# Cross-attention, 32 batches: in each window of the main loop the query products come first and third and the output products second and fourth, their two PSUM banks change places, and one query copy moves into the first softmax exponentials

## The chip, the cores and the metric

The kernel runs on one core of a Trainium2 chip. The metric is device time in microseconds (us) of one execution. The kernel before takes 1692.46 us, the median of three runs (1692.12 to 1692.76).

The core has a matrix engine (PE; its weight loads are listed apart as PEld), a vector engine (DVE), an activation engine (ACT), a general engine (POOL) and a queue that issues DMAs (SP). Each works through its own instructions in the order in which they stand. They wait for one another by semaphores.

## The reference: what is computed

```python
q = _heads(hidden_states @ to_q_w)
h_txt = _sdpa(q, _heads(ehs_txt @ to_k_w), _heads(ehs_txt @ to_v_w))
...
out = out @ to_out_w + to_out_b
out = (out + residual) / RESCALE
```

`x` is 32 batches of 512 rows by 640 columns, the context 32 batches of 77 rows by 1024. The attention has 20 heads of width 32. The context has only 77 rows, so the three further attentions of the source get empty slices and nothing of them is left: one attention, its output product, bias and residual are what must be computed. All is float32.

## The kernel before

**Pieces.** The 640 columns are cut into five pieces of 128 (four heads each). One *slot* is one piece of one batch, so there are N = 160 slots; slot n belongs to batch n // 5. A large product is made of 15 matmuls of 128x512: five pieces k of the inner dimension, and for each k three products of high and low parts (both operands are split into a rounded high part and the rest, the low part). The order is the same for every k: high·high, then weight high by **data low**, then weight low by data high (`PAIRS`). Counted from 0, matmul 3k+1 is the first to need the low part of piece k of the data.

**Stages.** A first part (about 320 us) makes keys and values of all batches and works off slots 0 to 7. The main loop, `window(n)`, then takes two slots at a time, n = 8, 10, ... 158: 76 windows. The position w = n % 10 says which batch work a window does beside its own, since two batches are ten slots.

**A window.** On PE stand, in this order:
- `values(n-4)` into bank `po` and `values(n-3)` into bank `pq` (L553): probabilities times values.
- `scores_of_two(n)` (L454): 64 small matmuls into the four `sc` banks and two `pa` banks.
- four large products of 15 matmuls: `group(early)` (L602, output product of slot n-8 into `po`), `queries(n+2)` (L437, into `pq`), `group(later)` (L602, into `po`), `queries(n+3)` (L437, into `pq`).

ACT casts the high parts of the two value results (`high_a`, L567), makes 32 exponentials with their sums (`exps`, L515), and copies the query product of slot n+2 to `qt` (`copy_q`, L449). DVE makes low parts (`low_a`, L572), row maxima (L508), the transposes of an output product (`turn`, L612), the reciprocal of the sums (L525), the transpose of the probabilities (`transpose_p`, L534) and the query copy of slot n+3 (L449). POOL multiplies the probabilities by the reciprocals (`normalize`, L527), adds output products to the residual (`add`, L616, after `turn`), adds the bias (`bias_of`, L587) and makes the low parts of x (`split_x`, L259, whose high part ACT casts in L258). SP issues `move_p` (L543) and the loads and stores.

**Batch work by position.** `split_x` makes the query operand `xt` of a batch, five pieces c = 0 to 4, at three places:
- w = 6: pieces 0 and 1 of batch b+2, late in the window.
- w = 8: pieces 2 to 4 of batch b+2, at the window's start. The first query product that reads them is `queries(n+2)` of this same window, since n+2 is the first slot of that batch.
- w = 2: pieces 0 and 1 of batch b+1 ahead of the exponentials, pieces 2 to 4 behind `normalize(n)`. The first query product that reads them is `queries(n+3)` of this same window.

`bias_of` runs in windows with w = 0, 4, 6 and 8. No scheduler moves anything: the order of each engine is the order in which the code calls the helpers.

Of the kernel before, what the change touches and what calls it, by code (L numbers as in the profile page):

```python
# [37 lines left out]
def kernel(  # L38
# [25 lines left out]
    nc = tc.nc  # L64
# [4 lines left out]
    NC_ = C // P  # L69
# [3 lines left out]
    N = B * NC_  # L73
# [176 lines left out]
    def split_x(b, c, high=nc.scalar.copy, low=nc.gpsimd):  # L250

        if b == 1 and c > 1:
            xt = xpool[1].tile([P, 2, S], FPR, tag="xu", name="xu", bufs=3)
        else:
            xt = xpool[0].tile([P, 2, S], FPR, tag="xt", name="xt", bufs=7)
        src = xss[b].rearrange("p (a t) u -> p t a u", t=NQ)[:, :, :, c * Q : (c + 1) * Q]
        parts = [xt[:, i, :].rearrange("p (t a j) -> p t a j", t=NQ, j=Q) for i in range(2)]
        high(parts[0], src)  # L258
        low.tensor_tensor(parts[1], src, parts[0].bitcast(F32), ALU.subtract)  # L259
        xts[b, c] = xt  # L260
# [26 lines left out]
    early = kvt.tile([P, P], F32, name="early", bufs=1)  # L287
# [144 lines left out]
    def queries(n, tag="pq"):  # L432
        b, j = divmod(n, NC_)
        pqs[n] = bank(tag)
        for k in range(NC_):
            for m, (a, c) in enumerate(PAIRS):
                nc.tensor.matmul(  # L437
                    pqs[n],
                    wq_s[:, k, a, j * P : (j + 1) * P],
                    xts[b, k][:, c, :],  # L440
                    start=(k == 0 and m == 0),
                    stop=(k == NC_ - 1 and m == 2),
                )
# [4 lines left out]
    def copy_q(n, copy=nc.scalar.copy):  # L448
        copy(qt_of(n), pqs.pop(n))  # L449
# [73 lines left out]
    def normalize(n):  # L523
        rs = main.tile([P, NQ * HPC], F32, tag="rs", name="rs", bufs=2)
        nc.vector.reciprocal(rs, sms.pop(n))  # L525
        pf = pnb[n % 2][:, :, :NKEY]
        nc.gpsimd.tensor_tensor(  # L527
            pf, pf, rs.unsqueeze(2).to_broadcast([P, NQ * HPC, NKEY]), ALU.mult
        )
# [18 lines left out]
    def values(n, tag="pa"):  # L548
        b, j = divmod(n, NC_)
        raw, vb = raws.pop(n), vbs[b % 2][:, j]  # L550
        pas[n] = bank(tag)
        for i in range(HPC):
            nc.tensor.matmul(  # L553
                pas[n][i * HD : (i + 1) * HD, :].rearrange("p (a q) -> p a q", q=P),
                vb[:, i, :],
                raw[:, :, i, :],
                start=True,
                stop=True,
                tile_position=(0, i * HD),
            )  # L560
# [35 lines left out]
    def group(b, c, ks, tag="po"):  # L596

        for k in ks:
            if k == 0:
                pos[b, c] = bank(tag)  # L600
            for m, (a, d) in enumerate(PAIRS):
                nc.tensor.matmul(  # L602
                    pos[b, c],
                    wos[0][:, k, a, c * P : (c + 1) * P],
                    ats[b * NC_ + k][:, d, :],
                    start=(k == 0 and m == 0),
                    stop=(k == NC_ - 1 and m == 2),
                )

    def turn(b, c):  # L610
        ots[b, c] = late[0].tile([P, S], F32, tag="ot", name="ot", bufs=2)
        nc.vector.transpose(ots[b, c], pos.pop((b, c)))  # L612

    def add(b, c):
        part = ys[b][:, :, c * Q : (c + 1) * Q]
        nc.gpsimd.tensor_tensor(  # L616
            part, part, ots.pop((b, c)).rearrange("p (a i) -> p a i", i=Q), ALU.add
        )
# [39 lines left out]
    def take(m, tag="pa"):  # L658
        values(m, tag)
        high_a(m)  # L660
        low_a(m)
# [65 lines left out]
    def window(n):  # L727

        w, b = n % 10, n // 10 * 2
        ahead = n + 2 < N  # L730
        taken = (n - 4, n - 3)
        early, later = (divmod(n - FIRST + i, NC_) for i in range(2))
        for m in taken:
            values(m, "pq" if m == n - 3 else "po")
        for m in taken:
            high_a(m)
        normalize(n - 1)
        for m in taken[:-1]:
            low_a(m)
        views, shared = scores_of_two(n)  # L740
        low_a(n - 3)
        for i in range(3):
            maxima_of(views[i], i)
        transpose_p(n - 1)
        maxima_of(views[3], 3)
        move_p(n - 2)
        if w == 8 and b:
            store_y(b - 1, range(4))
        if w == 8 and b + 2 < B:
            for c in range(2, NC_):  # L750
                split_x(b + 2, c)
        if w == 2:
            for c in range(2):
                split_x(b + 1, c)
        for i in range(HPC):
            exps(n, i)
        group(*early, range(NC_))
        turn(*early)
        for i in (1, 3):
            maxima_of(shared[i], i, 6)  # L760
        add(*early)
        move_p(n - 1)
        if w == 0:
            load_values(b)
            load_keys(b + 1)
            load_y(b - 1, range(4))
        if w == 2 and b > 1:
            store_y(b - 2, range(4))
        if w == 4:
            load_values(b + 1)  # L770
            if b + 2 < B:
                load_x(b + 2)
        if w == 6:
            if b + 2 < B:
                load_keys(b + 2)
            load_y(b, range(4))
        if w == 8 and b + 3 < B:
            load_x(b + 3)
        if ahead:
            queries(n + 2)  # L780
        normalize(n)
        if n == N - 10:
            nc.gpsimd.dma_start(biases[0], bo.unsqueeze(0).to_broadcast([P, C]))
        if w in BIAS and b >= BIAS[w][0]:
            for i in BIAS[w][1]:
                bias_of(b - BIAS[w][0], i)
        for i in (0, 2):
            exps(n + 1, i, range(2, NQ))
        if ahead:
            copy_q(n + 2)  # L790
        if w == 2:
            for c in range(2, NC_):
                split_x(b + 1, c)
        if w in (0, 6) and b + w // 6 + 1 < B:
            for i in range(NQ):
                transpose_x(b + w // 6 + 1, i)
        transpose_p(n)
        for i in (1, 3):
            exps(n + 1, i, range(2, NQ))
        for i in (1, 3, 0, 2):  # L800
            if i == 0 and w == 6 and b + 2 < B:
                for c in range(2):
                    split_x(b + 2, c)
            if i == 0 and not ahead:
                closing(n)
            exps(n + 1, i, range(2))
        if ahead:
            group(*later, range(NC_))
            turn(*later)
            add(*later)  # L810
            queries(n + 3)
            copy_q(n + 3, nc.vector.tensor_copy)

    def closing(n):

        last = B - 1
        for t in range(NQ):
            load_residual(t)
        for c, tag in ((1, "pq"), (2, "po")):
            group(last - 1, c, range(NC_), tag)  # L820
            turn(last - 1, c)
            add(last - 1, c)
        values(n - 2, "pq")
        high_a(n - 2)

    def end():


        last = B - 1
        low_a(N - 4)  # L830
        move_p(N - 2)
        normalize(N - 1)
        take(N - 3, "po")
        for c, tag in ((3, "pq"), (4, "po")):
            bias_of(last - 1, c - 2)
            group(last - 1, c, range(NC_), tag)
            turn(last - 1, c)
            if c == 3:
                transpose_p(N - 1)
                move_p(N - 1)  # L840
            add(last - 1, c)
        bias_of(last - 1, 3)
        store_y(last - 1, range(4))
        for t in range(NQ):
            add_bias(t)

        def begin(i, ks=range(4)):
            t, h = divmod(i, 2)
            if 0 in ks:
                pos[t, h] = bank(("sc", "sc", "sc", "sc", "pq", "po", "pa", "pa")[i])  # L850
            for k in ks:
                project(t, h, k)

        def close(t):
            for h in range(2):
                project(t, h, 4)
                finish(t, h)

        for i in range(4):
            begin(i, range(3))  # L860
        for m in (N - 2, N - 1):
            take(m)
        for i in (4, 5):
            begin(i, range(3))
        for i in range(6):
            begin(i, (3,))
        close(0)
        close(1)
        begin(6)
        close(2)  # L870
        begin(7)
        close(3)
# [68 lines left out]
```

## Time and profile before

| | |
|---|---|
| median of three runs | 1692.46 us |
| the profiled execution | 1692.86 us |
| its span (first to last instruction) | 1690.8 us |
| PE busy (matmuls) | 1683.6 us, 12460 matmuls |
| ACT busy | 1075.9 us |
| DVE busy | 1010.5 us |
| POOL busy | 990.1 us |
| one window at position w = 8 (n = 88), start to start | 17.63 us |

The profile is of one execution. A timeline row gives the start, the time until the last instruction of the row ends, the engine, the line, the operation, what is written and read, and how many instructions the row joins; in brackets stands the idle time of the engine ahead of it and what ended that. Two neighbouring instructions of one engine overlap a little, so the distance of two starts says better than the length how long an engine is taken. PE's busy time counts modelled ends and hides short waits; there too the distance of starts is read.

### The profile page before, as it was taken

The numbers are of one execution on the slowest core, as the hardware profiler recorded it, in microseconds if no ns is written. First come the engines' busy times: TensorE is split into PE (matmuls) and PEld (weight loads), VectorE is DVE, ScalarE is ACT, GpSimd is POOL, SyncE is SP. The second block draws the span as 40 slices with busy tenths as digits, with TensorE's granted clock in tenths as the row PEclk, the third lists the DMA queues.
The fourth block names the chain that finished last, engine by engine and source line by source line (L and its number), as shares of the span: only waits on it lengthen the run. The fifth ranks groups of instructions, "written<-read, shape, count | busy, mean of one in ns | idle before, by whom it ended". The sixth has DMA issues, their size and how long they took to land.

```text
span 1690.8 us, 36827 instructions
## 1 busy us (share of the span) xinstructions
PE 1683.6 (100%) x12460; PEld 1303.9 (77%) x12460; DVE 1010.5 (60%) x1635; ACT 1075.9 (64%) x5622; POOL 990.1 (59%) x663
## 2 busy tenths in 40 slices
PE   9999999999999999999999999999999999999999
PEld 7888898777777777777777777777777777777777
DVE  4341235766676666766666657576666766667653
ACT  3231125867677676776767767677676776767762
POOL 1000026667667666667575766767667676766755
PEclk9999999999999999999999999999999999999999
DMA  9847558678889787879797988888979788888956
GB/s 182 159 94 189 121 103 229 150 173 188 190 187 204 172 204 175 202 181 212 166 211 166 211 181 195 185 194 186 203 173 204 173 202 190 188 192 183 210 136 187
DMA packets 363852, 306.51 MB, mean 181 GB/s; under 512 B 88784, under 2 KB 292112, under 8 KB 363664
## 3 DMA queue, kind: packets, MB, share of 16 engines
q1 hardware_dynamic: 360864, 296.61, 78.4%
q0 software_dynamic: 2704, 7.38, 1.4%
q8 instruction: 99, 1.62, 0.4%
q14 instruction: 89, 0.73, 0.1%
q10 hardware_dynamic: 96, 0.16, 0.0%
HBM read 120.36 MB, written 57.88 MB: 105 GB/s over the span
## 4 chain that ended last, share of the span: by engine, by line
PE 97%; DMA 1%; ACT 0%; DVE 0%; SPq 0%; issue 0%; POOL 0%; DVEq 0%; ACTq 0%
PE pq L437 32%; PE po L602 31%; PE pv L182 7%; PE pk L182 7%; PE sc L454 6%; PE po L553 4%; PE pq L553 4%; PE pa L454 3%; DMA wraw<-in_L_xattn_to_k_w_dram 1%; PE sc L634 1%; PE pa L553 0%; ACT pn L515 0%; DMA cs<-in_ctx_dram 0%; PE pa L634 0%; PE pq L602 0%; SPq L99 0%
## 5 line engine op out<-in xcount | busy, mean ns | idle before, releaser
L515 ACT ACTIVATE pn<-sc,nm 128x77 f32<-128x77 f32 x1928 | 597.3, 367 | 131.4 <-DVE nm L508 102.8
L437 PE MATMUL pq<-xt,wq_s 128*128 128x512 f32 x2349 | 559.0, 390 | 0.0
L602 PE MATMUL po<-at,wo_s 128*128 128x512 f32 x2295 | 554.6, 393 | 0.0
L437 PEld LDWEIGHTS pq<-xt,wq_s 128*128 128x128 f32 x2349 | 440.6, 188 | 91.4
L602 PEld LDWEIGHTS po<-at,wo_s 128*128 128x128 f32 x2295 | 425.1, 188 | 90.8
L515 ACT ACTIVATION_READ_ACCUMULATOR pn<-sc,nm 128x1 f32 x1928 | 477.3, 249 | 0.0
L527 POOL TENSOR_TENSOR pn<-pn,rs 128x1232 f32<-128x1232 f32 x160 | 363.6, 2273 | 125.3 <-DVE rs L525 121.8
L616 POOL TENSOR_TENSOR xs<-xs,ot 128x512 f32<-128x512 f32 x155 | 199.8, 1289 | 322.1 <-DVE ot L612 314.4
L534 DVE STREAM_TRANSPOSE z<-pn 128x1536 f32<-128x1536 f32 x160 | 282.3, 1765 | 113.7 <-POOL pn L527 92.2
L259 POOL TENSOR_TENSOR xt<-xs,xt 128x512 fp32r<-128x512 f32 x157 | 198.5, 1293 | 35.8 <-ACT xt L258 35.8
L515 ACT ACTIVATE pn<-pa,nm 128x77 f32<-128x77 f32 x620 | 200.5, 382 | 0.0
L587 POOL TENSOR_TENSOR xs<-xs,bias_y 128x640 f32<-128x640 f32 x124 | 192.4, 1574 | 0.2
L567 ACT CAST at<-po 128x512 fp32r<-128x512 f32 x77 | 45.1, 585 | 230.1 <-PE po L553 230.1
L508 DVE TENSOR_REDUCE nm<-sc 128x6 f32<-128x462 f32 x304 | 177.1, 624 | 15.2 <-PE pa L454 15.2
L449 DVE COPY qt<-pq 128x512 f32<-128x512 f32 x83 | 57.4, 691 | 210.1 <-PE pq L437 210.1
L454 PE MATMUL sc<-kb,qt 32*128 32x77 f32 x3856 | 161.9, 273 | 0.0
L515 ACT ACTIVATION_READ_ACCUMULATOR pn<-pa,nm 128x1 f32 x620 | 161.0, 263 | 0.0
L454 PEld LDWEIGHTS sc<-kb,qt 32*128 32x128 f32 x3856 | 149.4, 187 | 4.2 <-issue 2.2
L182 PE MATMUL pk<-ct,wk_s 128*128 128x512 f32 (+1 forms) x600 | 134.0, 382 | 0.7 <-ACT wk_s L89 0.5
L182 PE MATMUL pv<-ct,wv_s 128*128 128x512 f32 (+1 forms) x600 | 134.2, 382 | 0.0
L454 PEld LDWEIGHTS pa<-kb,qt 32*128 32x128 f32 x1240 | 83.9, 186 | 63.7 <-ACT at L567 63.7
L182 PEld LDWEIGHTS pk<-ct,wk_s 128*128 128x128 f32 x600 | 112.1, 188 | 20.9 <-ACT wk_s L89 1.2
(81 smaller groups left out, 1339.7 us busy)
## 6 DMA issues: line engine op xcount, KB each, us to landing
raw<-z SPq DMA_DIRECT2D x640, 192.0 KB, 3.4
xs<-in_x_dram SPq DMA_DIRECT2D x256, 320.0 KB, 6.3
out_dram<-xs SPq DMA_DIRECT2D x127, 320.0 KB, 4.8
vb<-v_dram SPq DMA_DIRECT2D x32, 240.0 KB, 4.4
kb<-k_dram SPq DMA_DIRECT2D x32, 192.5 KB, 4.6
cs<-in_ctx_dram SPq DMA_DIRECT2D x12, 512.0 KB, 9.0
k_dram<-ks POOLq DMA_DIRECT2D x20, 256.0 KB, 2.5
v_dram<-vs SPq DMA_DIRECT2D x80, 64.0 KB, 2.4
```

Of the source, the lines that this page charges most:

```text
L182: nc.tensor.matmul(held[j][:, :gn], w[:, k, a, :], cts[g, k][:, c, :gn], start=(k == 0 and n == 0), stop=(k == NK - 1 and n == 2),)
L259: low.tensor_tensor(parts[1], src, parts[0].bitcast(F32), ALU.subtract)
L437: nc.tensor.matmul(pqs[n], wq_s[:, k, a, j * P : (j + 1) * P], xts[b, k][:, c, :], start=(k == 0 and m == 0), stop=(k == NC_ - 1 and m == 2),)
L454: nc.tensor.matmul(out, qt_of(n)[r, t * P : (t + 1) * P], kbs[b % 2][r, j, :], start=True, stop=True, tile_position=(i * HD, 0),)
L508: nc.vector.tensor_reduce(nm, view, AX.X, ALU.max, negate=True)
L515: nc.scalar.activation(pnb[n % 2][:, at, :NKEY], scs.pop((n, i, t)), AF.Exp, bias=nms.pop((n, i, t)), accum_out=sms[n][:, at : at + 1],)
L527: nc.gpsimd.tensor_tensor(pf, pf, rs.unsqueeze(2).to_broadcast([P, NQ * HPC, NKEY]), ALU.mult)
L534: nc.vector.transpose(z.rearrange("p c h t j -> p (h t) c j"), pn.rearrange("p a (c i) -> p a c i", i=Q),)
L553: nc.tensor.matmul(pas[n][i * HD : (i + 1) * HD, :].rearrange("p (a q) -> p a q", q=P), vb[:, i, :], raw[:, :, i, :], start=True, stop=Tru ...
L587: nc.gpsimd.tensor_tensor(part, part, biases[1].unsqueeze(1).to_broadcast([P, 4, U]), ALU.add)
L602: nc.tensor.matmul(pos[b, c], wos[0][:, k, a, c * P : (c + 1) * P], ats[b * NC_ + k][:, d, :], start=(k == 0 and m == 0), stop=(k == NC_ - ...
L616: nc.gpsimd.tensor_tensor(part, part, ots.pop((b, c)).rearrange("p (a i) -> p a i", i=Q), ALU.add)
```

## The change

In `window`: `queries(n+2)` is called right behind the scores and writes `po`; the copy of its result on ACT stands behind the third of the four heads' exponentials (`i == 2`) instead of behind the first exponentials of the second slot. `group(early)` follows as second and writes `pq`. Its `turn` comes behind the last two row maxima, not ahead of them. Its `add` on POOL is called behind `normalize(n)` instead of ahead of it, except at w = 2, where it stays ahead (the store of that batch follows there). At the window's end `queries(n+3)` (into `po`) and its copy on DVE come ahead of `group(later)` (into `pq`), its `turn` and `add`. `closing` and `end`, which run once, follow the swapped banks. No instruction is added or taken away.

```diff
         if w == 2:
             for c in range(2):
                 split_x(b + 1, c)
+        if ahead:
+            queries(n + 2, "po")
         for i in range(HPC):
             exps(n, i)
-        group(*early, range(NC_))
-        turn(*early)
+            if ahead and i == 2:
+                copy_q(n + 2)
         for i in (1, 3):
             maxima_of(shared[i], i, 6)
-        add(*early)
+        group(*early, range(NC_), "pq")
+        turn(*early)
+        if w == 2:
+            add(*early)
         move_p(n - 1)
...
-        if ahead:
-            queries(n + 2)
         normalize(n)
+        if w != 2:
+            add(*early)
...
         for i in (0, 2):
             exps(n + 1, i, range(2, NQ))
-        if ahead:
-            copy_q(n + 2)
...
         if ahead:
-            group(*later, range(NC_))
+            queries(n + 3, "po")
+            copy_q(n + 3, nc.vector.tensor_copy)
+            group(*later, range(NC_), "pq")
             turn(*later)
             add(*later)
-            queries(n + 3)
-            copy_q(n + 3, nc.vector.tensor_copy)
...
-        for c, tag in ((1, "pq"), (2, "po")):
+        for c, tag in ((1, "po"), (2, "pq")):
...
-        values(n - 2, "pq")
+        values(n - 2)
...
-        take(N - 3, "po")
+        take(N - 3)
```

The order on PE in a window with w = 2, behind the scores (names: `xt` the split x, `wq_s` the query weight, `at` the split attention output, `wo_s` the output weight; in brackets the semaphores that the first instruction of the row waits for). Before:

```order
L602 MATMUL po<-at,wo_s 128x512 [waits PE_49]
L602 MATMUL po<-at,wo_s 128x512 x14
L437 MATMUL pq<-xt,wq_s 128x512 [waits DVE_49,PE_49]
L437 MATMUL pq<-xt,wq_s 128x512 x14
L602 MATMUL po<-at,wo_s 128x512 [waits DVE_49]
L602 MATMUL po<-at,wo_s 128x512 x8
L602 MATMUL po<-at,wo_s 128x512 [waits Activation_49]
L602 MATMUL po<-at,wo_s 128x512 x2
L602 MATMUL po<-at,wo_s 128x512 [waits Activation_49]
L602 MATMUL po<-at,wo_s 128x512 x2
L437 MATMUL pq<-xt,wq_s 128x512 [waits Activation_49]
L437 MATMUL pq<-xt,wq_s 128x512 [waits Pool_49]
```

And with the change:

```order
L437 MATMUL po<-xt,wq_s 128x512 [waits PE_49]
L437 MATMUL po<-xt,wq_s 128x512 x14
L602 MATMUL pq<-at,wo_s 128x512 [waits DVE_49,PE_49]
L602 MATMUL pq<-at,wo_s 128x512 x14
L437 MATMUL po<-xt,wq_s 128x512 [waits Activation_49]
L437 MATMUL po<-xt,wq_s 128x512 [waits Pool_49]
L437 MATMUL po<-xt,wq_s 128x512 x2
L437 MATMUL po<-xt,wq_s 128x512 [waits Pool_49]
```

The query product whose matmuls each wait for a low part from POOL was the fourth large product and is now the third.

The order on POOL from the middle of a window with w = 6 into the next one with w = 8 (`xs<-xs,ot` is an `add`, `pn<-pn,rs` a `normalize`, `xs<-xs,bias_y` a bias, `xt<-xs,xt` a low part of x). Before:

```order
L616 TENSOR_TENSOR xs<-xs,ot 128x16x32
L527 TENSOR_TENSOR pn_1871<-pn_1871,rs 128x16x77
L587 TENSOR_TENSOR xs<-xs,bias_y 128x640 x2
L259 TENSOR_TENSOR xt<-xs,xt 128x512 x2
L616 TENSOR_TENSOR xs<-xs,ot 128x16x32
L527 TENSOR_TENSOR pn_1873<-pn_1873,rs 128x16x77
L259 TENSOR_TENSOR xt<-xs,xt 128x512 x3
```

And with the change:

```order
L527 TENSOR_TENSOR pn_1871<-pn_1871,rs 128x16x77
L616 TENSOR_TENSOR xs<-xs,ot 128x16x32
L587 TENSOR_TENSOR xs<-xs,bias_y 128x640 x2
L259 TENSOR_TENSOR xt<-xs,xt 128x512 x2
L616 TENSOR_TENSOR xs<-xs,ot 128x16x32
L527 TENSOR_TENSOR pn_1873<-pn_1873,rs 128x16x77
L259 TENSOR_TENSOR xt<-xs,xt 128x512 x3
```

One `add` moved from ahead of `normalize(n)` to behind it, into the run of instructions that ends with the three low parts of w = 8.

The order on DVE of a window without batch work, from its last row maxima of the `sc` banks to the end. Before:

```order
L508 TENSOR_REDUCE nm<-sc 128x6
L612 STREAM_TRANSPOSE ot<-po 128x512
L508 TENSOR_REDUCE nm<-pa 128x2 x2
L525 RECIPROCAL rs<-sm 128x16
L534 STREAM_TRANSPOSE z_1877<-pn_1871 128x16x3x32
L612 STREAM_TRANSPOSE ot<-po 128x512
L449 COPY qt_2665<-pq 128x512
```

And with the change:

```order
L508 TENSOR_REDUCE nm<-sc 128x6
L508 TENSOR_REDUCE nm<-pa 128x2 x2
L612 STREAM_TRANSPOSE ot<-pq 128x512
L525 RECIPROCAL rs<-sm 128x16
L534 STREAM_TRANSPOSE z_1877<-pn_1871 128x16x3x32
L449 COPY qt_2665<-po 128x512
L612 STREAM_TRANSPOSE ot<-pq 128x512
```

The `turn` of the early group, which reads the second large product of the window instead of the first, now stands directly ahead of the reciprocal, which `normalize(n)` on POOL waits for. The query copy and the `turn` of the later group have changed places.

## The prediction

> **What bounds the kernel now.** I read the page's busy times first, then the chain that ended last.
>
> ```profile
> PE 1683.6 (100%) x12460; PEld 1303.9 (77%) x12460; DVE 1010.5 (60%) x1635; ACT 1075.9 (64%) x5622; POOL 990.1 (59%) x663
> ...
> PE 97%; DMA 1%; ACT 0%; DVE 0%; SPq 0%; issue 0%; POOL 0%; DVEq 0%; ACTq 0%
> ```
>
> PE carries 97% of the chain. Modelled ends can hide short waits, so next I read the starts on PE in one window with w = 8 (n = 88) and, behind it, the two last products of one with w = 2 (n = 92).
>
> ```profile
> 1026.53 1.06 PE L553 MATMUL po<-raw,vb 96*32 96x512 f32 x8
> ...
> 1030.34 3.70 PE L602 MATMUL po<-at,wo_s 128*128 128x512 f32 x15
> ...
> 1037.27 3.56 PE L602 MATMUL po<-at,wo_s 128*128 128x512 f32 x15
> 1040.67 3.56 PE L437 MATMUL pq<-xt,wq_s 128*128 128x512 f32 x15
> 1044.16 1.06 PE L553 MATMUL po<-raw,vb 96*32 96x512 f32 x8
> ...
> 1072.51 3.56 PE L602 MATMUL po<-at,wo_s 128*128 128x512 f32 x15
> 1075.91 3.56 PE L437 MATMUL pq<-xt,wq_s 128*128 128x512 f32 x15
> ```
>
> A window is 1044.16 - 1026.53 = 17.63 us. A large product takes 1040.67 - 1037.27 = 3.40 us, a matmul 3.40 / 15 = 0.2267 us; the first product behind the scores takes about 0.14 more (3.70 against 3.56). No bracket with idle time stands in these rows. PE is full, so moving work cannot win more than crumbs: what matters is whether PE still finds every operand ready. Before, nothing on PE waited for POOL worth naming, because the low parts of x came just in time:
>
> ```profile
> 1018.90 2.28 POOL L527 TENSOR_TENSOR pn<-pn,rs 128x1232 f32<-128x1232 f32 x1 [0.19 <-DVE rs L525]
> 1021.14 3.12 POOL L587 TENSOR_TENSOR xs<-xs,bias_y 128x640 f32<-128x640 f32 x2
> 1024.20 2.57 POOL L259 TENSOR_TENSOR xt<-xs,xt 128x512 fp32r<-128x512 f32 x2
> 1026.69 1.32 POOL L616 TENSOR_TENSOR xs<-xs,ot 128x512 f32<-128x512 f32 x1
> 1027.93 2.30 POOL L527 TENSOR_TENSOR pn<-pn,rs 128x1232 f32<-128x1232 f32 x1
> 1030.16 3.81 POOL L259 TENSOR_TENSOR xt<-xs,xt 128x512 fp32r<-128x512 f32 x3
> ...
> 1036.54 2.27 POOL L527 TENSOR_TENSOR pn<-pn,rs 128x1232 f32<-128x1232 f32 x1 [0.19 <-DVE rs L525]
> ...
> 1070.33 1.29 POOL L616 TENSOR_TENSOR xs<-xs,ot 128x512 f32<-128x512 f32 x1 [2.74 <-DVE ot L612]
> 1071.81 2.28 POOL L527 TENSOR_TENSOR pn<-pn,rs 128x1232 f32<-128x1232 f32 x1 [0.19 <-DVE rs L525]
> 1074.03 3.80 POOL L259 TENSOR_TENSOR xt<-xs,xt 128x512 fp32r<-128x512 f32 x3
> ```
>
> These are POOL's rows from the window with w = 6 into w = 8 (1018.90 to 1033.97, not a gap in it), and in the window with w = 2. POOL is busy 59% on the whole but has no slack in these two places. In the window with w = 2 the last low part is there at 1074.03 + 3.80 = 1077.83; the matmul that needs it, number 13 of the product that starts at 1075.91, comes at 1075.91 + 13 x 0.2267 = 1078.86. That is 1.03 us of cover.
>
> **The change part by part.** Instructions and their lengths are the same; only places change.
>
> *Queries earlier.* `queries(n+2)` starts where the first product started, 3.5 us earlier; `queries(n+3)` starts 3.40 us earlier. In w = 2 this alone takes the 1.03 us of cover and leaves 2.4 us of waiting.
>
> *Normalize later.* `turn(early)` now waits for the second product of the window, and the reciprocal stands behind it. DVE's rows give the hand-overs:
>
> ```profile
> 1036.21 0.25 DVE L525 RECIPROCAL rs<-sm 128x16 f32<-128x16 f32 x1 [0.79 <-ACT pn L515]
> ...
> 1040.87 0.72 DVE L612 STREAM_TRANSPOSE ot<-po 128x512 f32<-128x512 f32 x1 [0.25 <-PE po L602]
> 1044.27 0.69 DVE L449 COPY qt<-pq 128x512 f32<-128x512 f32 x1 [2.68 <-PE pq L437]
> 1044.88 0.24 DVE L525 RECIPROCAL rs<-sm 128x16 f32<-128x16 f32 x1
> ```
>
> A `turn` starts 1040.87 - 1040.67 = 0.20 us behind the start of PE's next product, a reciprocal 0.61 us behind an instruction of this size (1044.88 - 1044.27), and `normalize` 0.33 us behind the reciprocal (1036.54 - 1036.21). In the window with w = 6 the second product ends at 1037.27 - 17.63 = 1019.64. So `turn` starts at 1019.84, the reciprocal at 1020.45, `normalize(n)` at 1020.78: **1.88 us later** than 1018.90. The copy that ACT now makes ahead of the fourth head (0.59 us) ends earlier than that and is hidden by this wait.
>
> *Add behind normalize.* Outside w = 2 the early `add` goes behind `normalize(n)`, into the stretch without a gap. POOL from w = 6 on, by the distances of the starts above: `normalize` 1020.78, `add` 1023.02, bias 1024.26 (an `add` takes 1027.93 - 1026.69 = 1.24), two low parts 1027.32, late `add` 1029.81, `normalize` 1031.05, three low parts from 1033.28, ready at 1034.55, 1035.82 and 1037.09. That is 1.88 + 1.24 = 3.12 us later than before.
>
> **Term 1, w = 8.** `queries(n+2)` starts at 1030.34; its matmul 7 comes at 1030.34 + 0.14 + 7 x 0.2267 = 1032.07 and needs the low part of 1034.55: a wait of 2.48. Then three matmuls take 0.68 while POOL takes 1.27 for a piece: two waits of 0.59. Sum 3.66, with the semaphores' passing 3.7 us. There are 14 such windows (n = 18 to 148; at n = 8 no window with w = 6 stands ahead, and the last one splits nothing): 14 x 3.7 = **52 us**.
>
> **Term 2, w = 2.** Here the early `add` stays ahead of `normalize(n)`, and both now stand behind the second product, which ends at 1072.51. `turn` runs from 1072.71 to 1073.43; the `add` starts at about 1073.57, `normalize` at 1074.81, the low parts at 1074.81 + 2.22 = 1077.03, ready at 1078.30, 1079.57 and 1080.83. `queries(n+3)` starts at 1072.51 and needs the first at matmul 7, at 1074.10: a wait of 4.20, and two more of 0.59. Sum 5.4 us. There are 15 such windows (n = 12 to 152): 15 x 5.4 = **81 us**.
>
> *Cheap parts.* `values(n-3)` waited for a bank that the query copy on DVE freed; it will wait for the later `turn`. Their mean lengths differ little:
>
> ```profile
> L449 DVE COPY qt<-pq 128x512 f32<-128x512 f32 x83 | 57.4, 691 | 210.1 <-PE pq L437 210.1
> ...
> L612 DVE STREAM_TRANSPOSE ot<-po 128x512 f32<-128x512 f32 x153 | 106.7, 698 | 10.3 <-PE po L602 10.2
> ```
>
> 7 ns in 76 windows is 0.5 us. `transpose_p(n)` comes 1.9 us later, and the query copy on DVE stands behind it; the window's fourth product (3.40 us) covers the copy. At the end one wait goes, 0.45 us, for the bank of `values(n-2)`:
>
> ```profile
> 1658.16 1.07 PE L553 MATMUL pq<-raw,vb 96*32 96x512 f32 x8 [0.45 <-DVE ot L612]
> ```
>
> These cancel; I count nothing. The `move_p` issues on SP follow `transpose_p` and have most of a window before their values are used.
>
> **Term 3, the clock.** Gaps of 2.5 to 4.2 us on PE are new, and the trace of before has none in the loop. Its ends show what one may do:
>
> ```profile
> 1.46 6.39 PE L269 MATMUL warm<-zero 128*128 128x512 f32 x15 [1.46 <-DVE zero L266]
> ...
> 1684.61 2.80 PE L634 MATMUL pa<-wo_s,at 128*128 128x320 f32 x18
> ...
> 1687.50:1690.00 2.50, 0.00 (x0) 0.00 (x0) 0.47 (x2) 0.00 (x0) 0.00 (x0) 1.00 0.38 131
> 1690.10:1690.70 0.60, 0.00 (x0) 0.00 (x0) 0.00 (x0) 0.00 (x0) 0.00 (x0) 0.50 0.00 0
> ```
>
> The last matmul ends at 1684.61 + 2.80 = 1687.41; the granted clock (third column from the right in the windows rows) still reads 1.00 up to 1690.00 and 0.50 from 1690.10, some 2.6 us after. At the start 15 matmuls take 6.39 us, about 0.43 each instead of 0.2267: the first ones ran at half speed for some 6 us. So a gap of 4.2 us probably drops the clock and one of 2.5 us perhaps not. If it stays low for 5.8 us behind the gap, the first 2.5 us cost nothing (three matmuls at 0.43 take 1.28 us, as long as POOL's piece), and half of the other 3.3 us is lost: 1.65. The bounds are 0 and 29 gaps x 1.65 = 48 us. I take two in three of the 15 long gaps, since 4.2 is well above 2.6 but a drop may also fall so late that little is lost: 10 x 1.65 = **16 us**.
>
> **Sum.** 52 + 81 + 16 = 149 on the profiled execution's own 1692.86 (span 1690.8, the rest around it); the median of runs is 0.4 below. 1692.9 + 149 = **1842 us**.
>
> **The rivals.**
> - *The clock stays full.* For it: full speed still holds 2.5 us behind the last matmul, and each gap is closed by matmuls. Against it: 4.2 is more than 2.6. Time 1692.9 + 133 = 1826. Chance 23%.
> - *The clock falls in the long gaps and comes back sooner,* after about the length of one product, 3.40 us: (3.4 - 2.5) / 2 = 0.45 in each of 15, 7 us. For it: behind the gap PE is soon full. Against it: at the start the low clock lasted about 6 us. Time 1692.9 + 133 + 7 = 1833. Chance 15%. The Trainium skill speaks for this case in "TensorE: Matmul & The Clock Gate", section "HAM oscillation — how this bites in real kernels": PE must not idle for more than about 3.4 us, or its clock is halved; by that rule the 15 long gaps drop and the short ones don't. The trace agrees on the halving, but shows it after 2.6 us.
> - *The clock falls in all 29 gaps.* For it: after a first wait of 2.5 us come two more. 1692.9 + 133 + 48 = 1874. Chance 10%.
> - *The late transposes become the bound.* In windows with w = 0 and 6 four transposes of x stand between reciprocal and `transpose_p(n)`; the query copy then ends less than 1 us ahead of the next `values`, which need its bank. If it is late by 0.5 us in 31 windows, 15 us come on top: 1857. Chance 4%.
> - *Nothing is late: not slower.* It needs the low parts on time: in w = 2 POOL would have to be 5.4 us earlier than worked out, that is, run the low parts ahead of `add` and `normalize`. The order on POOL speaks against it. Then only the crumbs are left: 1692.9 - 0.45 + 0.5, 1693, within 0.2% (what a measurement of this kernel can tell from no change). Chance 3%.
>
> **How the numbers follow.** The forecast, long gaps with a partial drop of the clock, has 45%, and 1842 is its time. The range 1820 to 1873 reaches from the full clock with terms 1 and 2 some 4% smaller to all 29 gaps; what it leaves out is the last rival, half of the third and the edges of the others, some 15%. Slower by over 0.2%: 97%; within: 2%; faster: 1%.
>
> **What would show it.** Windows with w = 2 start to start near 23 us and with w = 8 near 21.3, all others at 17.6. In PE's waits a new line, L437 waiting for POOL's `xt` of L259, of 100 us or more. POOL's `normalize(n)` 1.9 us later in the window. Slices of PEclk below 9, or matmul pitches of 0.43 us behind the long gaps, for term 3. It would be wrong if the windows with w = 8 kept 17.6 us (then POOL's run is not what I took it for), or if windows at w = 0, 4 or 6 grew.

## The result, and the profile after

The changed kernel takes **1850.34 us** (median of 4 runs, 1849.56 to 1851.15) against 1692.29 for the kernel before (median of 4): ratio 1.0934, 95% interval 1.0915 to 1.0953, 158 us more. The forecast was 1842, with 1820 to 1873 as its range. The profiled execution has a span of 1847.6 us.

The page of the changed kernel, busy times and the chain that ended last:

```profile
PE 1743.4 (94%) x12460; PEld 1325.4 (72%) x12460; DVE 1006.1 (54%) x1635; ACT 1072.5 (58%) x5622; POOL 985.0 (53%) x663
...
PE 83%; POOL 8%; issue 4%; DMA 3%; DVE 1%; SPq 1%; POOLq 0%; DVEq 0%
```

PE's share of the chain fell from 97% to 83%, and POOL, which had none, has 8%: PE now waits for POOL. PE is also "busy" 60 us longer for the same 12460 matmuls, which hints that some of them ran slower. The list of PE's waits names the line (columns: engine, what waits, for whom, us in total, times, longest):

```profile
PE po L437 <- POOL xt L259: 98.0, 42, 4.0
```

Query products wait for low parts of x, a line that before did not have. The timeline of PE from a window with w = 8 (n = 88, from 1107.75 to 1130.13) and of the third and fourth products of one with w = 2 (n = 92):

```profile
1107.75 1.06 PE L553 MATMUL po<-raw,vb 96*32 96x512 f32 x8
...
1111.58 1.89 PE L437 MATMUL po<-xt,wq_s 128*128 128x512 f32 x7
1115.92 0.97 PE L437 MATMUL po<-xt,wq_s 128*128 128x512 f32 x3 [2.45 <-POOL xt L259]
1117.15 2.50 PE L437 MATMUL po<-xt,wq_s 128*128 128x512 f32 x5 [0.26 <-POOL xt L259]
1119.45 3.94 PE L602 MATMUL pq<-at,wo_s 128*128 128x512 f32 x15
1123.24 3.56 PE L437 MATMUL po<-xt,wq_s 128*128 128x512 f32 x15
...
1158.52 1.76 PE L437 MATMUL po<-xt,wq_s 128*128 128x512 f32 x7
1164.31 3.73 PE L437 MATMUL po<-xt,wq_s 128*128 128x512 f32 x8 [4.02 <-POOL xt L259]
1167.84 3.69 PE L602 MATMUL pq<-at,wo_s 128*128 128x512 f32 x15
```

The break is where the prediction put it: after seven matmuls, ahead of number 7, which is the first to need the low part of piece 2. The first product of the window with w = 8 takes 1119.45 - 1111.58 = 7.87 us instead of 3.53, the third of the one with w = 2 takes 1167.84 - 1158.52 = 9.32 instead of 3.40. POOL's rows to these two breaks:

```profile
1101.99 2.28 POOL L527 TENSOR_TENSOR pn<-pn,rs 128x1232 f32<-128x1232 f32 x1 [7.31 <-DVE rs L525]
1104.22 1.30 POOL L616 TENSOR_TENSOR xs<-xs,ot 128x512 f32<-128x512 f32 x1
1105.61 3.09 POOL L587 TENSOR_TENSOR xs<-xs,bias_y 128x640 f32<-128x640 f32 x2
1108.66 2.51 POOL L259 TENSOR_TENSOR xt<-xs,xt 128x512 fp32r<-128x512 f32 x2
1111.13 1.29 POOL L616 TENSOR_TENSOR xs<-xs,ot 128x512 f32<-128x512 f32 x1
1112.38 2.26 POOL L527 TENSOR_TENSOR pn<-pn,rs 128x1232 f32<-128x1232 f32 x1
1114.61 3.71 POOL L259 TENSOR_TENSOR xt<-xs,xt 128x512 fp32r<-128x512 f32 x3
...
1159.52 1.29 POOL L616 TENSOR_TENSOR xs<-xs,ot 128x512 f32<-128x512 f32 x1 [3.20 <-DVE ot L612]
1160.76 2.27 POOL L527 TENSOR_TENSOR pn<-pn,rs 128x1232 f32<-128x1232 f32 x1
1162.99 3.73 POOL L259 TENSOR_TENSOR xt<-xs,xt 128x512 fp32r<-128x512 f32 x3
```

`normalize` in the window with w = 6 sits idle for 7.31 us until DVE's reciprocal and then starts a run without a gap that ends in the three low parts. In the w = 2 window `add` waits 3.20 us for its `turn`, and `normalize` and the low parts queue behind it.

The clock is read from stretches of the same trace (busy times of PE, PEld, DVE, ACT and POOL, then PEclk, DMA share, GB/s), ahead of the drop, in it and behind it, for both places:

```profile
1109.40:1116.70 7.30, 4.85 (x78) 3.60 (x74) 5.59 (x9) 6.00 (x29) 7.30 (x6) 1.00 0.85 195
1116.90:1120.10 3.20, 2.94 (x7) 2.27 (x8) 0.53 (x3) 0.41 (x1) 1.42 (x2) 0.50 0.91 247
1120.30:1127.00 6.70, 6.70 (x31) 5.55 (x30) 1.17 (x3) 6.13 (x40) 2.63 (x2) 1.00 1.00 233
...
1164.70:1167.90 3.20, 3.20 (x9) 2.10 (x8) 0.14 (x1) 0.00 (x0) 2.01 (x2) 0.50 0.83 217
```

The granted clock is 0.50 for about 3.4 us behind each of the two gaps. Over the whole run its mean is 0.973: 0.027 x 1847.6 / 0.5 = 100 us at half clock. The trace's record of the clock has 29 stretches of 3.41 us, one for each of the 29 gaps.

Start to start of the windows, means in us (w = 8 without the first window, n = 8):

| kernel | w = 8 (14) | w = 2 (15) | w = 0 | w = 4 | w = 6 | time | mean clock |
|---|---|---|---|---|---|---|---|
| before | 17.63 | 17.61 | 17.63 | 17.62 | 17.63 | 1692.3 | 1.000 |
| the change | 22.36 | 23.63 | 17.66 | 17.64 | 17.67 | 1850.3 | 0.973 |
| spare matmuls in the gaps | 21.55 | 23.16 | 17.66 | 17.64 | 17.66 | 1831.2 | 1.000 |
| fewer spare matmuls | 22.70 | 23.38 | 17.66 | 17.65 | 17.67 | 1849.9 | 0.983 |
| early splits in w = 2 | 22.15 | 18.26 | 17.66 | 17.63 | 17.67 | 1766.2 | 0.990 |
| all low parts ready | 17.93 | 17.75 | 17.66 | 17.63 | 17.67 | 1698.4 | 1.000 |
| reciprocal ahead of the turn | 20.15 | 22.45 | 17.66 | 17.65 | 17.67 | 1800.8 | 0.986 |
| late add in w = 6 | 20.15 | 24.15 | 18.07 | 17.65 | 17.67 | 1834.0 | 0.978 |
| old end in w = 2 | 22.85 | 19.73 | 17.66 | 17.63 | 17.66 | 1797.2 | 0.987 |
| query copy back | 21.09 | 24.05 | 18.46 | 18.47 | 18.47 | 1876.9 | 0.975 |

The change adds 14 x 4.73 = 66 us at w = 8 and 15 x 6.02 = 90 at w = 2; the other windows grow by 0.02 to 0.04 each (the first one, n = 8, by 0.42). That is the whole loss.

### The profile page after: what moved, and what is told of

Its sections match the earlier page's. It is cut to its first block, busy times and chain, and to the rows that moved or that the text cites. A ratio compares the mean times of both kernels' runs of the same rounds, so it can differ in the third digit from the quotient of the medians.

```text
span 1847.6 us, 36825 instructions
## 1 busy us (share of the span) xinstructions
PE 1743.4 (94%) x12460; PEld 1325.4 (72%) x12460; DVE 1006.1 (54%) x1635; ACT 1072.5 (58%) x5622; POOL 985.0 (53%) x663
## 4 chain that ended last, share of the span: by engine, by line
PE 83%; POOL 8%; issue 4%; DMA 3%; DVE 1%; SPq 1%; POOLq 0%; DVEq 0%
PE po L437 26%; PE pq L602 25%; PE pv L182 7%; PE pk L182 7%; PE sc L454 5%; PE po L553 4%; POOL pn L527 3%; POOL xt L259 3%; PE pq L553 3%; DMA raw<-z 3%; PE pa L454 2%; PE pq L437 2%; SPq L543 1%; DVE z L534 1%; POOL xs L616 1%
## 5 line engine op out<-in xcount | busy, mean ns | idle before, releaser
L437 PE MATMUL po<-xt,wq_s 128*128 128x512 f32 x2256 | 598.4, 416 | 98.1 <-POOL xt L259 98.0
L515 ACT ACTIVATE pn<-sc,nm 128x77 f32<-128x77 f32 x1928 | 612.0, 394 | 131.1 <-DVE nm L508 81.6
L437 PEld LDWEIGHTS po<-xt,wq_s 128*128 128x128 f32 x2256 | 430.9, 197 | 218.8 <-POOL xt L259 132.4
L602 PE MATMUL pq<-at,wo_s 128*128 128x512 f32 x2295 | 551.7, 392 | 0.0
L602 PEld LDWEIGHTS pq<-at,wo_s 128*128 128x128 f32 x2295 | 439.4, 192 | 95.3 <-DVE at L572 0.8
L515 ACT ACTIVATION_READ_ACCUMULATOR pn<-sc,nm 128x1 f32 x1928 | 500.6, 274 | 0.0
L612 DVE STREAM_TRANSPOSE ot<-pq 128x512 f32<-128x512 f32 x153 | 109.7, 717 | 342.1 <-PE pq L602 342.1
L515 ACT ACTIVATION_READ_ACCUMULATOR pn<-pa,nm 128x1 f32 x620 | 183.2, 311 | 0.0
L182 PEld LDWEIGHTS pv<-ct,wv_s 128*128 128x128 f32 x600 | 112.3, 188 | 19.6 <-ACT wv_s L89 0.3
```

What stands on the lines that cost most here:

```text
L182: nc.tensor.matmul(held[j][:, :gn], w[:, k, a, :], cts[g, k][:, c, :gn], start=(k == 0 and n == 0), stop=(k == NK - 1 and n == 2),)
L437: nc.tensor.matmul(pqs[n], wq_s[:, k, a, j * P : (j + 1) * P], xts[b, k][:, c, :], start=(k == 0 and m == 0), stop=(k == NC_ - 1 and m == 2),)
L515: nc.scalar.activation(pnb[n % 2][:, at, :NKEY], scs.pop((n, i, t)), AF.Exp, bias=nms.pop((n, i, t)), accum_out=sms[n][:, at : at + 1],)
L602: nc.tensor.matmul(pos[b, c], wos[0][:, k, a, c * P : (c + 1) * P], ats[b * NC_ + k][:, d, :], start=(k == 0 and m == 0), stop=(k == NC_ - ...
```

## The experiments

The theory: PE waits for POOL's low parts at two positions, and each wait halves the clock for a while. Rivals: the swapped banks, the moved `turn` and the moved copy cost by themselves; the clock costs nothing.

**Spare matmuls in the gaps.** Ahead of matmul 7 of the query products in question stand extra matmuls that write bank `pq`, which is free there; nobody reads their result.

```diff
+                if fill and (k, m) == (2, 1):
+                    spare = bank("pq")
+                    for _ in range(fill):
+                        nc.tensor.matmul(
+                            spare, wq_s[:, 0, 0, :P], xts[b, 0][:, 0, :], start=True, stop=True
+                        )
...
+    FILL8, FILL2 = 10, 17
...
-            queries(n + 2, "po")
+            queries(n + 2, "po", FILL8 if w == 8 and n > FIRST else 0)
...
-            queries(n + 3, "po")
+            queries(n + 3, "po", FILL2 if w == 2 else 0)
```

> The changed kernel with 10 spare matmuls (windows w = 8, but for the first) or 17 (w = 2) ahead of the matmul that waits for the first late low part; they write a bank whose result nobody reads, so the output stays as it was. Theory 'waits and clock': the waits are set by POOL and stay, the spare work fits into them (10 x 0.227 = 2.3 us of 2.6, 17 x 0.227 = 3.9 of 4.2), the granted clock stays at 1.00, and the time falls by what the half clock cost: w = 2 from 23.64 to about 23.05, w = 8 from 22.38 to about 21.35, in sum 15 x 0.6 + 14 x 1.05 = 24, so about 1826 us (1820 to 1832). Rival 'the half clock costs nothing, it only runs while PE is paced by POOL': 1850, or more.

Measured: 1831.23 us (ratio to before 1.0824, interval 1.0807 to 1.084), 19 us less than the change with 395 more matmuls. The timeline of PE in a window with w = 8 (here L440 is the spare work, L443 the query product), and the mean clock:

```profile
1102.22 1.89 PE L443 MATMUL po<-xt,wq_s 128*128 128x512 f32 x7
1103.94 2.43 PE L440 MATMUL pq<-xt,wq_s 128*128 128x512 f32 x10
1106.58 0.96 PE L443 MATMUL po<-xt,wq_s 128*128 128x512 f32 x3 [0.21 <-POOL xt L259]
1107.82 0.96 PE L443 MATMUL po<-xt,wq_s 128*128 128x512 f32 x3 [0.28 <-POOL xt L259]
1109.06 0.73 PE L443 MATMUL po<-xt,wq_s 128*128 128x512 f32 x2 [0.27 <-POOL xt L259]
```

```profile
core 0: 1829.1 us, clock 1.000
```

The query product is as long in waits as POOL makes it (three matmuls for each 1.24 us), but everything behind it runs at full clock. So the half clock costs 19 us, and the waits alone 139. The rival that the clock is free falls.

**Early splits in w = 2.**

```diff
         for i in range(HPC):
             exps(n, i)
+            if w == 2 and i == 1:
+                for c in range(2, NC_):
+                    split_x(b + 1, c)
...
-        if w == 2:
-            for c in range(2, NC_):
-                split_x(b + 1, c)
```

> The changed kernel, but in windows with w = 2 the three splits (pieces 2 to 4) are called behind the second head's exponentials, so that POOL makes their low parts in its idle time ahead of the early add. Theory 'waits for POOL': windows with w = 2 go back to 17.65 us, 15 x 6.0 = 90 us less, about 1760; windows with w = 8 keep their 22.4 (if they lose the clock drop, 1745). Rival 'the swapped banks and the moved turn cost in every window': 1850, no window changes.

Measured: 1766.17 us (1.042 to 1.0458), 84 us less. Windows with w = 2 lose the gap, but keep 0.6 us over the others. PE's waits tell why:

```profile
PE po L437 <- POOL xt L259: 37.9, 27, 2.5
PE po L553 <- DVE qt L449: 7.8, 15, 1.0
```

The first line is what is left at w = 8; there the first gap is as long as in the change (2.44 to 2.46 us), but only 10 of the 14 were followed by half clock. The second is new: the five low parts now stand in one run on POOL, `add` and `normalize(n)` come behind them, `transpose_p(n)` behind these, and the query copy on DVE behind that; the next window's first values wait 0.5 us for bank `po`. It is the rival of the late transposes, 15 times, in a place that the prediction had not named.

**All low parts ready.** The edit of the last run, and for w = 8:

```diff
         for m in taken:
             high_a(m)
+        if w == 8 and b + 2 < B:
+            for c in range(2, NC_):
+                split_x(b + 2, c)
         normalize(n - 1)
...
-        transpose_p(n - 1)
-        maxima_of(views[3], 3)
+        if w == 8:
+            maxima_of(views[3], 3)
+            transpose_p(n - 1)
+        else:
+            transpose_p(n - 1)
+            maxima_of(views[3], 3)
...
-        if w == 8 and b + 2 < B:
-            for c in range(2, NC_):
-                split_x(b + 2, c)
...
+        if w in BIAS and b >= BIAS[w][0]:
+            for i in BIAS[w][1]:
+                bias_of(b - BIAS[w][0], i)
         group(*early, range(NC_), "pq")
...
-        if w in BIAS and b >= BIAS[w][0]:
-            for i in BIAS[w][1]:
-                bias_of(b - BIAS[w][0], i)
```

> As the previous one, and for windows with w = 8: the bias of a window is called ahead of normalize(n) instead of behind it, and pieces 2 to 4 are split ahead of normalize(n-1) (with the last row maxima ahead of the transpose of the probabilities there). PE's order, banks and the place of the query copy are those of the changed kernel. Theory 'waits for POOL': all low parts are ready, no window is longer than 17.66, the clock stays at 1.00, and the time is that of the kernel before within 0.2%: 1693 to 1696 (1.5 us for a turn of 0.72 in place of a copy of 0.69 ahead of the second values). Rival 'banks, turn and copy cost by themselves': most of the 158 us stays, over 1750.

Measured: 1698.4 us (ratio 1.0039, interval 1.0026 to 1.0052). No wait for `xt` is left in PE's list, and the clock is 1.000. The first products of a window with w = 8 and of one with w = 2:

```profile
679.10 3.94 PE L437 MATMUL po<-xt,wq_s 128*128 128x512 f32 x15
682.88 3.61 PE L602 MATMUL pq<-at,wo_s 128*128 128x512 f32 x15
...
714.70 3.74 PE L437 MATMUL po<-xt,wq_s 128*128 128x512 f32 x15
718.27 3.56 PE L602 MATMUL pq<-at,wo_s 128*128 128x512 f32 x15
```

152 of the 158 us are gone with PE's new order, the swapped banks, the moved `turn` and the moved copy all in place, so these cost 6 us at most by themselves: the rival falls. The 6 us are more than expected. The windows are 7.5 us longer in sum: 14 x 0.30 at w = 8 (682.88 - 679.10 is 3.78 instead of 3.53: pauses too short for the list of waits), 15 x 0.14 at w = 2, 0.26 in the first window and up to 0.04 in the rest; the loop of this execution began 0.8 us earlier (320.70 against 321.52), which gives part of it back. The run beats the change but not the kernel before.

**Reciprocal ahead of the turn.**

```diff
         group(*early, range(NC_), "pq")
+        normalize(n)
         turn(*early)
...
-        normalize(n)
         if w != 2:
             add(*early)
```

> The changed kernel, but normalize(n) with its reciprocal is called ahead of turn(early), so that it doesn't wait for the second product. The last of the 16 exponentials ends some 1.3 us earlier than that turn, so normalize and the low parts behind it come about 1.3 us earlier in both places: 29 x 1.35 = 39 us less, 1811; if the shorter first wait in w = 8 (1.2 us) no longer drops the clock, 14 x 1.05 more, 1796. Rival 'normalize is not on the path, the late add or PE's order alone does it': 1850.

Measured: 1800.83 us (1.0624 to 1.0663), near the lower of the two. PE's first product in a window with w = 8:

```profile
800.45 1.89 PE L437 MATMUL po<-xt,wq_s 128*128 128x512 f32 x7
803.41 0.97 PE L437 MATMUL po<-xt,wq_s 128*128 128x512 f32 x3 [1.07 <-POOL xt L259]
804.65 0.97 PE L437 MATMUL po<-xt,wq_s 128*128 128x512 f32 x3 [0.28 <-POOL xt L259]
805.89 0.73 PE L437 MATMUL po<-xt,wq_s 128*128 128x512 f32 x2 [0.26 <-POOL xt L259]
```

The first wait falls from 2.45 to 1.07 us, and the two last matmuls run at full clock (0.73 us for two, where the change has 2.50 for five). The windows with w = 8 are 2.2 us shorter, 1.4 from the wait and the rest from the clock, which stays up there: its mean of 0.986 makes 0.014 x 1799.4 / 0.5 = 50 us at half clock, 15 stretches, those of w = 2. The windows with w = 2 are 1.2 us shorter (22.45 for 23.63): there `normalize` now fills the time in which POOL waited for the `turn`.

**Late add in w = 6.**

```diff
-        if w == 8 and b:
-            store_y(b - 1, range(4))
         if w == 8 and b + 2 < B:
             for c in range(2, NC_):
                 split_x(b + 2, c)
+        if w == 8 and n > FIRST:
+            add(*divmod(n - 2 - FIRST, NC_))
+        if w == 8 and b:
+            store_y(b - 1, range(4))
...
-        if w != 2:
+        if w not in (2, 6):
             add(*early)
```

> The changed kernel, but the early add of windows with w = 6 is put off until behind the three low parts of the next window (ahead of the store that needs it). POOL's run without a gap gets 1.24 us shorter, so the waits in w = 8 fall from 3.66 to 2.4 and the first of them to 1.2, too short to drop the clock by what the run with the early normalize showed: w = 8 from 22.4 to 20.1, 14 x 2.3 = 32 us less, 1818; 1833 if the clock still falls there. Rival 'the add was not in the run that matters': 1850.

Measured: 1834.01 us (1.0805 to 1.0868), 16 us less, where 32 were expected. At w = 8 the step is right to the tenth (20.15). But half of it is given back: w = 0 grows by 0.41 us and w = 2 by 0.52. For w = 0 the lists of PE and of SP's queue name the way:

```profile
PE pq L553 <- DMA raw<-z: 3.5, 10, 1.2
```

```profile
SPq L594 <- POOL xs L616: 129.5, 30, 6.7
```

The store of y (L594) now waits on SP for the late `add`, 129.5 us in all against 46.7 with the change, and the `move_p` issued behind it brings the values' operand late. For w = 2 it is the clock: of its 15 drops 9 last 6.83 us, twice 3.41, and these windows take 24.59 us in the mean, the 6 others 23.48. One such stretch (0.50 is the clock):

```profile
762.60:769.30 6.70, 5.44 (x13) 4.11 (x14) 2.47 (x2) 1.35 (x10) 3.67 (x3) 0.50 0.62 154
```

Why they last longer there stays open.

**Old end in w = 2.**

```diff
+            if w == 2:
+                group(*later, range(NC_), "po")
+                turn(*later)
+                add(*later)
+                queries(n + 3, "pq")
+                copy_q(n + 3, nc.vector.tensor_copy)
+            else:
+                queries(n + 3, "po")
...
```

> The changed kernel, but windows with w = 2 end as before: output group (into po), then queries(n+3) (into pq). The query product starts 3.40 us later there, while POOL's low parts come as late as in the changed kernel: the waits fall from 5.4 to 2.0, the clock stays up there, w = 2 goes from 23.63 to 19.6, 15 x 4.0 = 60 us less, about 1790. Rival 'the order on PE is without blame, the gap comes from elsewhere': 1850.

Measured: 1797.24 us (1.0588 to 1.065), 53 us less. At w = 2 the window falls to 19.73, as expected; the longest wait there is 0.7 us:

```profile
PE pq L437 <- POOL xt L259: 16.5, 38, 0.7
```

The difference to the expected 60 is at w = 8, which grew by 0.5 us each (all 14 gaps still drop the clock there, but later: 4.4 us behind the gap's start in the mean, where the change has 3.3). At full clock w = 2 lost 5.5 us (23.16 for 17.65): 3.4 of them go with PE's order (23.16 - 19.73), and the 2.1 that stay come from POOL's.

**Query copy back.**

```diff
         for i in range(HPC):
             exps(n, i)
-            if ahead and i == 2:
-                copy_q(n + 2)
...
         for i in (0, 2):
             exps(n + 1, i, range(2, NQ))
+        if ahead:
+            copy_q(n + 2)
```

> The changed kernel with the query copy on ACT back where it stood before, behind the first exponentials of the second slot. Theory 'the copy frees po for the third product': in the kernel before the copy ran from 10.94 to 11.53 us of a window, but the third product now starts at 10.63, so PE waits some 0.95 us in each window with w = 0, 4 and 6 (at w = 2 and w = 8 the waits for low parts cover it): 45 x 0.95 = 43 us more, about 1893. Rival 'where the copy stands doesn't matter': 1850. Rival 'the copy amid the exponentials is what delays normalize': 1830 or less.

Measured: 1876.87 us (1.1057 to 1.1122), 27 us more. A new line stands among PE's waits, and windows with w = 0, 4 and 6 grow by 0.81 us:

```profile
PE po L437 <- ACT qt L449: 30.2, 60, 0.8
```

45 x 0.81 = 36 us, where 43 were expected, and 0.42 more at w = 2, where 7 of the 15 drops of the clock last 6.83 us. No theory had said that 1.27 a window comes back at w = 8 (21.09 for 22.36). The trace shows how: PE takes 0.80 us longer for the window with w = 6, while POOL's `normalize` still starts 11.90 us into it (11.89 with the change). So the low parts are less late, the first wait at w = 8 is 1.63 us instead of 2.45, and only 5 of these 14 gaps drop the clock. The copy amid the exponentials is what lets `queries(n+3)` have bank `po` in time, and it does not delay `normalize`.

**Fewer spare matmuls.**

```diff
-    FILL8, FILL2 = 10, 17
+    FILL8, FILL2 = 3, 10
```

> As the run with spare matmuls, but with 3 (w = 8) and 10 (w = 2) of them: they leave some 1.75 us of idle PE at one piece in each gap, where the changed kernel had 2.45 and 4.0 and the run with early normalize had a first gap in w = 8 of about 1.2 without a drop. If a drop needs an idle stretch of over 2 us: no drop, 1831 as with the full filling. If 1.75 us is enough: up to 29 drops, 1840 to 1850.

Measured: 1849.92 us (1.0899 to 1.0962), mean clock 0.983:

```profile
core 0: 1848.4 us, clock 0.983
```

0.017 x 1848.4 / 0.5 = 63 us at half clock, 18 stretches for 29 gaps of 1.74 to 1.78 us: all 14 at w = 8, and 4 of 15 at w = 2. Neither branch fits: gaps of one length drop the clock in some places and not in others, and spare work that leaves them gains nothing (1849.9 for 1850.3).

## Why the prediction was right, point by point

- *PE is full; only late operands matter.* Right: with all operands ready the new order costs 6 us of 158.
- *Normalize 1.88 us later.* Right: 1101.99 is 11.89 us into the window with w = 6, against 10.01 before.
- *Term 1, w = 8: 52 us.* At full clock the window is 21.55, 3.9 us over the others: 55 us. The three low parts start 1114.61 - 1107.75 = 6.86 us into the window, predicted 6.75. Late `normalize` and `add` both work as said: each, taken back alone, shortens w = 8 by 2.2 us, clock included.
- *Term 2, w = 2: 81 us.* At full clock 5.5 us over the others: 83 us. The low parts start at 15.20 us, predicted 15.23.
- *Term 3, the clock: 16 us.* Measured 19, but from other factors than the prediction's 10 drops of 1.65 us. All 29 gaps dropped, the short ones too, as in the rival that had 10%, and the clock came back after 3.4 us, as in the rival that had 15%; one drop cost 19 / 29 = 0.66. The two errors nearly cancel. The forecast was wrong in both parts of this term, and that their product came out near 19 is luck.
- *Cheap parts: nothing.* The scores start 0.99 us behind the second values instead of 0.97, 76 x 0.02 = 1.5 us in all, where 0.5 minus 0.45 was reckoned.
- *The rivals.* "Nothing is late" did not occur. With the clock kept full by spare work the time was 1831.2, where that rival had 1826. The late transposes did nothing here, and showed up in the run with early splits.

The 1842 fell 8 us short: 3, 2 and 3 us from terms 1 to 3; the 1.5 us of the cheap parts and the profiled execution's 0.6 us over the median nearly cancel.

## What to carry to other kernels

On a full engine an order is as good as the slack of what feeds it: before a consumer is moved forward, find the last producer of each of its operands and follow that producer's queue back to where it last was idle. An engine that is busy 53% on average can have a run of 16 us with hardly a gap exactly there, and whatever is put into that run arrives in full at its end. Where a wait can't be avoided, work that nobody needs can keep the clock up: here 395 spare matmuls made the kernel 19 us faster. They had to fill the wait: with 1.75 us of it left idle, nothing was won.

## What the runs showed of the hardware

An idle stretch of PE of 2.45 us was followed by half clock in all 14 windows with w = 8 of the change. In the place shown the clock still read 1.00 up to 1116.70 and 0.50 from 1116.90, when PE had been at work again since 1115.92; it lasted 3.41 us. The rule of about 3.4 us in "TensorE: Matmul & The Clock Gate" of the Trainium skill, section "HAM oscillation — how this bites in real kernels", which the prediction weighed, would have spared the gaps of 2.45; the measurement decides.

The length of a gap alone does not decide. In the run with early splits 4 of the 14 gaps of this same length were followed by no drop. Here is one of them, and one with a drop; under PE's row that ends the gap stands a stretch behind the start of this gap, with the clock as the third number from the right:

```profile
604.80 0.96 PE L437 MATMUL po<-xt,wq_s 128*128 128x512 f32 x3 [2.45 <-POOL xt L259]
602.00:612.00 10.00, 7.00 (x29) 4.89 (x28) 3.57 (x6) 7.03 (x45) 5.22 (x4) 1.00 0.91 240
...
697.49 0.96 PE L437 MATMUL po<-xt,wq_s 128*128 128x512 f32 x3 [2.44 <-POOL xt L259]
699.40:702.60 3.20, 3.19 (x8) 2.16 (x7) 0.00 (x0) 1.38 (x7) 0.51 (x1) 0.50 0.88 248
```

Gaps of 1.75 us dropped it in 18 of 29 cases; with the reciprocal ahead of the turn, where the first wait at w = 8 is 1.07 us, none of the 14 did. What the drops share is a grid: within each run all of them start whole multiples of 3.413 us apart (in the change the first three at 372.7, 423.9 and 471.7 us, 15 and 14 steps). In the run with early splits the four gaps without a drop begin 2.0 us behind a line of this grid, the ten others 1.0 to 1.2 or 2.5 to 2.9 us behind one. Why the place on the grid decides, no run shows.

The drops also make the windows fall into step with the grid: five windows of the change take 22.36 + 23.63 + 17.66 + 17.64 + 17.67 = 98.96 us, 29 steps of 3.413; with the reciprocal ahead of the turn they take 95.58, 28 steps; with the spare matmuls, which leave no drop, 97.67, no whole number of steps.

And where a drop falls sets its price. A window with w = 8 of the run with early splits takes 21.53 us without a drop, 21.98 when the drop begins 2.4 us behind the gap's start, and 22.80 at 4.2; in the change it is 22.36 at 3.3. An estimate from the rows of the change gives the same: POOL paces PE until 2.45 + 1.24 + 1.24 = 4.93 us behind the gap's start, and half of what the 3.41 us reach beyond that is lost, 0.44 for a drop at 2.4, 0.89 at 3.3 and 1.35 at 4.2, where 0.45, 0.83 and 1.27 were measured. That accounts for the half microsecond by which w = 8 grew where the old end mended only w = 2: its drops begin at 4.4, which the estimate puts at 0.55 us more than 3.3; measured are 0.49 (22.85 for 22.36).
